# A graph layer on one core: weights in 13 loads instead of 51, blocks laid out on chip, and the first runs' rows turned a run ahead

## The chip, the cores and the metric

The kernel runs on one core of a Trainium2 chip. The metric is the device time of one execution in microseconds, lower is better. A core has five engines with a queue of instructions each: PE (matrix products and transposes), ACT (activations, here mostly copies out of PSUM), DVE (elementwise work), POOL (here: the gathers) and SP (here: issues DMAs). DMAs can be issued from SP, ACT and POOL. Engines wait for one another and for DMAs through semaphores.

## The reference

There are 12,500 nodes with 128 numbers each and 412,500 edges, sorted by destination. Each edge has a source node, 4 attributes (`edge_attr_4`) and 8 radial numbers (`edge_attr_8`).

```python
f0 = x0 @ W1_0e / sqrt(32)                         # x0 = x[:, :32],  x1 = the other 96 as (32, 3)
f1 = einsum('nui,uw->nwi', x1, W1_1o) / sqrt(32)
feat0, self0 = f0[:, :32], f0[:, 32:]              # likewise feat1, self1
e0, e1 = feat0[src], feat1[src]
h = gelu(edge_attr_8 @ W_mlp1 / sqrt(8)); h = gelu(h @ W_mlp2 / sqrt(64))
w00, w01, w10, w11 = h @ Wp_00, h @ Wp_01, h @ Wp_10, h @ Wp_11
mid = products of w.., e0, e1 and the 4 edge attributes        # scalar and vector parts
n0, n1 = segment_sum(mid, dst) / sqrt(32)
conv = n0 @ W2_0e, n1 @ W2_1o (scaled)
out = layernorm(x + cos(pi/8) * self + sin(pi/8) * conv)
```

## The kernel before

**Edges.** The sorted edges are cut into 806 runs of 512 (`SB`), a run into 4 quarters of 128 (one edge per partition), and four runs form a chunk (`CH`).

**Node features.** The features of all nodes are computed once and written to a table in HBM. This is the loop over 25 groups of 512 nodes (`NG`): `load_nodes` brings a group from SP (L156), `turn` transposes it on PE (L180) and ACT copies it into the accumulator `acc` (L181), `features_of` multiplies by the weight `wf` on PE (L187), DVE copies the result (L190), and `store_nodes` writes it to `table` from ACT's queue (L164). Three `xt` and three `ft` buffers and four PSUM buffers `w` let the groups overlap. Half way, `load_indices(0)` turns the source and destination indices of the first 128 runs on PE and DVE.

**Gathers.** `gather(s)` fetches the source rows of a run with one indirect DMA per quarter on POOL (L124), so four per run. It runs up to 19 runs ahead of the work (`LEAD` = 20 buffers `G`). The first 16 runs (`RAW`) don't wait for the table: they gather rows of `x` itself. Their rows are then transposed and multiplied by `wf` when their turn comes, in `features(s)`. In one run of 14 (`AID`), from run 36 on, the fourth quarter is brought by SP instead, as 128 loads of one row (L116).

**The loop over runs.** For run s it does, on PE: now and then a step of the edge MLP (`radial`, `mlp1`, `mlp2`: L347, L356, L371) for a later chunk and `weights` (L388) for two later runs; `segments(s - 1)` (L434), which sums the messages of a run into windows of nodes by a product with the selection `S`; for a raw run `features(s)` (L395 transposes, ACT copy L397, L400 products, ACT copy L402). DVE does `messages(s)` (L422, L425) and `placing(s)`. Per chunk follow `place`, `project` and `add` into `acc`; finished nodes are normalised and stored by `norm`.

**What sets the order.** PE, ACT, DVE and SP execute in the order written in the program (`manual_schedule`); POOL's gathers and a few instructions outside that block, such as the copy of `first_node` (L746), are placed by the scheduler. A `G` buffer becomes free when the last reader is done: for a raw run that is the transposes L395, for another the messages.

**Weights.** `load_wf` fills the block weight `wf` with four loads from ACT's queue, and ACT scales it (L660). `weight_loads` yields 47 more loads (16 of them place `W_mlp1` block by block into `w1b`; the three of `ws` write single floats three apart); the node loop issues three of them from SP per group (L677). After the loop, SP loads the edge data of chunks 1 to 3 (L338) and `aid_rows` (L105), `scale_weights` scales `ws` on ACT and builds `wpost` on DVE, and then come the first steps of the edge MLP, `weights(0)`, `select(0)` and `set_floor`, 25 memsets on DVE (L255, L258), before the loop over runs begins.

Of the kernel before, what the change touches and what calls it, by code (L numbers as in the profile page):

```python
# [49 lines left out]
def gnn_kernel(ctx: ExitStack, tc: tile.TileContext, x, src, dst, ea4, ea8, w1_0, w1_1, wm1, wm2,  # L50
# [114 lines left out]
        if tail:  # L165
            eng.dma_start(dest[n0 + full * P:n0 + nn, :], t[:tail, full, :])

    def load_wf(eng):
        nc.vector.memset(wf, 0.0)
        eng.dma_start(wf[:MUL, :MUL], w1_0[:, :MUL])  # L170
        for i in range(3):
            eng.dma_start(wf[MUL + i::3, MUL + MUL * i:MUL + MUL * (i + 1)], w1_1[:, :MUL])

    XT, PX, PF = {}, {}, {}

# [26 lines left out]
    ones = cst.tile([P, 1], F32)  # L202
    first_node = cst.tile([1, NS], I32)

    def clear():
        for t in (w1b, ws, wpost):
            nc.vector.memset(t, 0.0)
        nc.vector.memset(acc[:, N:], 0.0)
        nc.vector.memset(ones, 1.0)

    def weight_loads():

        for h in range(2):
            for k in range(CH // 2):
                for q in range(Q):
                    r = h * HID + k * Q * RAD + q * RAD
                    yield w1b[r:r + RAD, k * 2 + q // 2, (q % 2) * HID:(q % 2 + 1) * HID], wm1
        for h in range(2):
            rows = slice(h * HID, (h + 1) * HID)
            yield w2b[rows, :], wm2  # L220
            for j, w in enumerate((wp00, wp01, wp10, wp11)):
                yield wpb[rows, j * MUL:(j + 1) * MUL], w
        yield w20[:MUL, :], w2_0[:MUL, :]
        yield w21[:MUL, :], w2_1[:MUL, :]
        for i in range(3):
            r = slice(MUL * (i + 1), MUL * (i + 2))
            yield w20[r, :], w2_0[MUL:, :]
            yield w21[r, :], w2_1[MUL:, :]
        yield first_node, sub(dst, 0, [[1, 1], [SB, NS]])
        yield ws[:MUL, :MUL], w1_0[:, MUL:]  # L230
        for i in range(3):
            yield ws[MUL + i::3, MUL + i::3], w1_1[:, MUL:]

    def scale_weights():
        nc.scalar.mul(ws, ws, math.cos(MIX) / math.sqrt(MUL))
        post = math.sin(MIX) / math.sqrt(2.0) / math.sqrt(NEIGHBORS) / math.sqrt(2 * MUL)
        nc.vector.tensor_scalar(wpost[:MUL, 0, :MUL], w20[:MUL, :], post, None, op0=OP.mult)
        for i in range(3):
            r = slice(MUL * (i + 1), MUL * (i + 2))
            nc.vector.tensor_scalar(wpost[r, 0, MUL + i::3], w21[r, :], post, None, op0=OP.mult)  # L240
            nc.vector.tensor_scalar(wpost[:MUL, 1 + i, MUL + i::3], w21[:MUL, :], post, None, op0=OP.mult)
            nc.vector.tensor_scalar(wpost[r, 1 + i, :MUL], w20[r, :], post / math.sqrt(3.0), None, op0=OP.mult)
# [38 lines left out]
    def load_raws(b):  # L281
        raws[b] = [load_run_rows(dst, b, NO_NODE), load_run_rows(src, b, 0)]
# [42 lines left out]
    def load_edges(b):  # L325
        s0 = b * CH
        ns = min(CH, NS - s0)
        e4[b] = wk.tile([P, CH, Q, 4], F32, name="e4", bufs=EDGES_AHEAD)
        e8[b] = wk.tile([P, CH, Q, RAD], F32, name="e8", bufs=EDGES_AHEAD)
        part = s0 + ns == NS and REM < SB  # L330
        fl = ns - 1 if part else ns
        if part:
            nc.vector.memset(e4[b][:, fl], 0.0)
        if fl < CH:
            nc.vector.memset(e8[b][:, fl:], 0.0)
        for a, t, n in ((ea8, e8[b], RAD), (ea4, e4[b], 4)):
            if fl:
                nc.sync.dma_start(t[:, :fl].rearrange("p s q k -> p (s q) k"),  # L338
                                  sub(a, s0 * SB * n, [[n, P], [P * n, fl * Q], [1, n]]))
            if part and RQ:  # L340
                nc.sync.dma_start(t[:, fl, :RQ, :], sub(a, (s0 + fl) * SB * n, [[n, P], [P * n, RQ], [1, n]]))
            if part and RP:
                nc.sync.dma_start(t[:RP, fl, RQ, :], sub(a, ((s0 + fl) * SB + RQ * P) * n, [[n, RP], [1, n]]))
# [44 lines left out]
                nc.tensor.matmul(WP[i][:, q, :], H2[c][q % 2][rows, k, q // 2, :], wpb[rows, :],  # L388
                                 start=True, stop=True)

    def features(s):

        pt = ps.tile([P, Q, P], F32, name="h")
        for q in range(Q):
            nc.tensor.transpose(pt[:, q, :], G[s][:, q, :], ident)  # L395
        xr = wk.tile([P, Q, P], F32, name="xt", bufs=3)
        nc.scalar.activation(xr, pt, AF.Copy)  # L397
        pf = ps.tile([P, Q, P], F32, name="h")
        for q in range(Q):
            nc.tensor.matmul(pf[:, q, :], xr[:, q, :], wf, start=True, stop=True)  # L400
        G[s] = wk.tile([P, Q, P], F32, name="ft", bufs=3)
        nc.scalar.activation(G[s], pf, AF.Copy)  # L402

# [245 lines left out]

    with tc.manual_schedule(engines={PE, ACT, DVE, SP}):  # L650
        load_raw_rows(nc.sync, 0, min(2, raw_runs))
        load_wf(nc.scalar)
        if raw_runs > 2:
            load_raw_rows(nc.scalar, 2, raw_runs)
        for s in range(min(LEAD - 2, raw_runs)):
            gather(s)
        nc.vector.tensor_scalar(ident, diag, 0.0, None, op0=OP.is_equal)
        for b in range(min(3, NG)):
            XT[b] = load_nodes(b)
        nc.scalar.mul(wf, wf, 1.0 / math.sqrt(MUL))  # L660
        clear()
        nc.vector.memset(odd, 0.0)
        loads = weight_loads()
        for b in range(NG + 2):
            if b == 1:
                load_edges(0)
                load_raws(0)
            if b < NG:
                turn(b)
            if 0 < b <= NG:  # L670
                features_of(b - 1)
            if 1 < b:
                store_nodes(nc.scalar, table, b - 2, PF[b - 2])
            if b + 3 < NG:
                XT[b + 3] = load_nodes(b + 3)
            for _, (to, of) in zip(range(3), loads):
                nc.sync.dma_start(to, of)  # L677
            if b == NG // 2:
                load_indices(0)
        for to, of in loads:  # L680
            nc.sync.dma_start(to, of)
        for c in range(1, min(EDGES_AHEAD, NCH)):
            load_edges(c)
        scale_weights()
        if aided:
            aid_load()
        for s in range(min(LEAD - 2, raw_runs), min(LEAD - 1, NS)):
            gather(s)
        selfs, loaded = list(range(NG)), {}
        radial(0)  # L690
        mlp1(0)
        mlp2(0)
        if NCH > 1:
            radial(1)
            mlp1(1)
        weights(0)
        select(0)
        set_floor()
        for s in range(NS + 1 + CH):
            c, k = divmod(s, CH)  # L700
            if s + LEAD - 1 < NS:
                gather(s + LEAD - 1)
            if k == 3 and c + EDGES_AHEAD < NCH:
                load_edges(c + EDGES_AHEAD)
            if s % P == P // 2 - 16 and (s // P + 1) * P < NS:
                load_raws(s // P + 1)
            if s % P == P // 2 and (s // P + 1) * P < NS:
                load_indices(s // P + 1)
            for t in range(P // ROWS):
                a = s + AID_LEAD - t * STEPS // (P // ROWS)  # L710
                if a in aided:
                    aid(a, t)
            if k == 0 and c + 1 < NCH:
                mlp2(c + 1)
            if k == 1 and c + 2 < NCH:
                radial(c + 2)
            if k % 2 == 0 and s + 2 < NS:
                weights(s + 2)
            if k == 3 and c + 2 < NCH:
                mlp1(c + 2)  # L720
            if k == 2 and 0 < c <= NCH:
                project(c - 1)
            if 0 < s <= NS:
                segments(s - 1)
            if k == 1 and 0 < c <= NCH:
                place(c - 1)
            if s < NS:
                if s < raw_runs:
                    features(s)
                messages(s)  # L730
                placing(s)
            if k == 2 and 0 < c <= NCH:
                add(c - 1)
                norm(due.get(c - 1, []), last=c == NCH)
            if k == 3 and c + 1 < NCH:
                select(c + 1)
            if selfs and s + 8 >= self_from and (s + 8) % self_every == 0:
                b = selfs.pop(0)
                loaded[s + 8] = b, load_nodes(b)
            if s in loaded:  # L740
                self_part(*loaded.pop(s))
        assert not selfs and not loaded
# [41 lines left out]
```

## Time and profile before

| | us |
|---|---|
| median of 3 runs | 6025.94 (6022.07 to 6031.2) |
| the profiled execution | 4038.2 |
| its span, first to last instruction | 4036.1 |
| busy: PE | 3087.6 |
| busy: POOL | 2994.5 |
| busy: DVE | 1718.0 |
| busy: ACT | 1025.7 |
| granted PE clock, mean | 0.761 |

The profile shows one execution, and its time is well under the runs' median. A row of a group gives the line, the engine, the operation, the tile written and the tiles read, the count, the busy time and the mean of one, then the idle time of the engine before it and what ended most of that. In a timeline a row begins with the start and the duration in us; the brackets at its end give the engine's idle time before it and who ended it. An engine name with a q is the engine's queue (SPq: SP issuing DMAs). "issue" is idle time in which the engine waited for nothing that the profile shows.

### The profile page before, as it was taken

What the parts mean: (1) busy time and instruction counts of PE and PEld (TensorE: products, weight loads), DVE (VectorE), ACT (ScalarE), POOL (GpSimd) and SP (SyncE); (2) the same over time, 40 slices, a digit from 0 to 9 for tenths busy, and PEclk for the clock granted to TensorE, in tenths of its full rate; (3) what the DMA queues carried; (4) which work ended last, traced back from release to release, by engine and by line L of the source; (5) the groups of instructions that cost most, each with busy time, mean ns of one, the idle gap of its engine ahead of it and who ended that gap; (6) DMA issues with size and microseconds to landing.
All of it is one profiled execution on the core that took longest, in us unless ns stands there. A gap on an engine that the chain in (4) does not pass through costs nothing.

```text
span 4036.1 us, 82179 instructions
## 1 busy us (share of the span) xinstructions
PE 3087.6 (77%) x25199; PEld 2188.4 (54%) x25199; DVE 1718.0 (43%) x4937; ACT 1025.7 (25%) x2264; POOL 2994.5 (74%) x3176
## 2 busy tenths in 40 slices
PE   5787778777787777778777778877777777777876
PEld 5565455555555555555555555555555555555554
DVE  2354545434444444444344443444444444444343
ACT  2232322322322222222222222222222222222222
POOL 6567777777777777777777777777777777777775
PEclk7787888787877777777777777777777777777776
DMA  8223333333333333333333333333333333333331
GB/s 186 43 53 68 67 73 68 74 68 74 70 69 63 59 66 66 59 66 59 59 64 66 60 62 62 60 64 65 60 64 61 61 60 65 61 60 65 61 59 47
DMA packets 1014835, 265.84 MB, mean 66 GB/s; under 512 B 904975, under 2 KB 962072, under 8 KB 1014386
## 3 DMA queue, kind: packets, MB, share of 16 engines
q0 software_dynamic: 101408, 207.89, 19.9%
q1 hardware_dynamic: 892687, 46.18, 13.8%
q10 hardware_dynamic: 20290, 6.45, 0.6%
q8 instruction: 201, 3.29, 0.3%
q14 instruction: 249, 2.03, 0.2%
HBM read 247.45 MB, written 12.80 MB: 64 GB/s over the span
## 4 chain that ended last, share of the span: by engine, by line
POOL 40%; issue 27%; DMA 11%; PE 10%; DVE 6%; SPq 4%; ACT 2%; DVEq 0%; POOLq 0%; ACTq 0%
POOL G L124 40%; DMA G<-table,idx 9%; SPq L116 2%; PE w L388 2%; DVE M L425 2%; PE seg L434 1%; PE m L459 1%; PE h L371 1%; PE m L451 1%; DMA xt<-in_x 1%; PE m L450 1%; ACT y L520 1%; DVE acc L468 1%; SPq L112 1%; DMA e<-in_edge_attr 1%
## 5 line engine op out<-in xcount | busy, mean ns | idle before, releaser
L124 POOL DMA_INDIRECT G<-table,idx x3105 | 2932.8, 945 | 993.2 <-issue 877.3
L422 DVE TENSOR_TENSOR M<-w,G 128x256 f32<-128x256 f32 x790 | 334.8, 424 | 1800.0 <-DMA G<-table,idx 1600.6
L388 PE MATMUL w<-wpb,h 64*128 64x128 f32 x6448 | 777.0, 358 | 210.1 <-DVE M L425 209.2
L434 PE MATMUL seg<-M,S 128*32 128x256 f32 x6448 | 615.9, 459 | 408.1 <-DVE M L425 393.5
L388 PEld LDWEIGHTS w<-wpb,h 64*128 64x128 f32 x6448 | 633.8, 249 | 371.8 <-DVE M L425 255.0
L425 DVE TENSOR_TENSOR M<-w,G 128x384 f32<-128x384 f32 x1580 | 799.7, 548 | 0.0
L437 ACT ACTIVATE sg<-seg 128x256 f32<-128x256 f32 x806 | 310.5, 385 | 1804.8 <-PE seg L434 1796.3
L451 PE MATMUL m<-pl,sg 128*128 128x96 f32 x1612 | 493.2, 401 | 0.0
L434 PEld LDWEIGHTS seg<-M,S 128*32 128x32 f32 x6448 | 141.7, 117 | 546.9 <-issue 436.9
L371 PE MATMUL h<-h,w2b 64*64 64x256 f32 x3232 | 331.4, 419 | 108.9 <-ACT h L360 102.6
L450 PEld LDWEIGHTS m<-pl,sg 128*128 128x128 f32 x1612 | 350.4, 268 | 113.6 <-issue 85.9
L450 PE MATMUL m<-pl,sg 128*128 128x32 f32 x1612 | 376.2, 322 | 0.0
L459 PE MATMUL m<-st,wpost 128*128 128x128 f32 (+1 forms) x1616 | 374.8, 405 | 1.2 <-ACT st L453 1.2
L451 PEld LDWEIGHTS m<-pl,sg 128*128 128x128 f32 x1612 | 362.3, 277 | 0.0
L459 PEld LDWEIGHTS m<-st,wpost 128*128 128x128 f32 x1616 | 322.8, 297 | 41.8 <-issue 34.7
L371 PEld LDWEIGHTS h<-h,w2b 64*64 64x64 f32 x3232 | 145.4, 141 | 291.7 <-ACT h L360 232.6
L356 PEld LDWEIGHTS h<-eT,w1b 64*128 64x128 f32 x3232 | 233.1, 217 | 121.6 <-issue 110.6
L376 ACT ACTIVATE h<-h 128x512 f32<-128x512 f32 x404 | 219.2, 595 | 260.3 <-PE h L371 260.3
L356 PE MATMUL h<-eT,w1b 64*128 64x128 f32 x3232 | 273.7, 315 | 9.3 <-ACT eT L349 8.3
L443 DVE TENSOR_SCALAR pl<-iota,colv 128x128 f32<-128x128 f32 x806 | 237.0, 294 | 94.3 <-PE m L451 91.5
L360 ACT ACTIVATE h<-h 128x512 f32<-128x512 f32 x404 | 219.2, 594 | 163.6 <-PE h L356 159.0
L453 ACT ACTIVATE st<-m 128x512 f32<-128x512 f32 x202 | 120.4, 596 | 503.4 <-PE m L451 503.4
(101 smaller groups left out, 1178.4 us busy)
## 6 DMA issues: line engine op xcount, KB each, us to landing
G<-table SPq DMA_DIRECT2D x7040, 0.5 KB
G<-table,idx POOLq DMA_INDIRECT x3105
e<-in_edge_attr SPq DMA_DIRECT2D x201, 64.0 KB
xt<-in_x SPq DMA_DIRECT2D x48, 256.0 KB
e<-in_edge_attr SPq DMA_DIRECT2D x201, 32.0 KB
table<-ft ACTq DMA_DIRECT2D x24, 256.0 KB
out<-y SPq DMA_DIRECT2D x24, 256.0 KB
raw<-in_dst SPq DMA_DIRECT2D x6, 256.0 KB
```

The source lines that it names most:

```text
L124: nc.gpsimd.indirect_dma_start(out=G[s][:, q, :], out_offset=None, in_=x if s < raw_runs else table, in_offset=bass.IndirectOffsetOnAxis(a ...
L356: nc.tensor.matmul(p1[h][:, j // 2, j % 2, :], w1b[rows, j, :], eT[c][rows, :], start=True, stop=True)
L371: nc.tensor.matmul(p2[r][k * HID:(k + 1) * HID, h * n:(h + 1) * n], w2b[rows, :], H1[c][h][rows, k * n:(k + 1) * n], start=True, stop=True)
L388: nc.tensor.matmul(WP[i][:, q, :], H2[c][q % 2][rows, k, q // 2, :], wpb[rows, :], start=True, stop=True)
L422: nc.vector.tensor_tensor(m[:, :, :, :MUL], w[:, :, :2 * MUL].rearrange("p q (a u) -> p q a u", a=2), g[:, :, None, :MUL].to_broadcast([P, ...
L425: nc.vector.tensor_tensor(m[:, :, j, MUL:].rearrange("p q (i u) -> p q i u", i=3), w[:, :, None, (2 + j) * MUL:(3 + j) * MUL].to_broadcast ...
L434: nc.tensor.matmul(pt[q * W:(q + 1) * W, :], S[c][:, r * Q + q].rearrange("p k j -> p (k j)"), M[s][:, q].rearrange("p a u -> p (a u)"), s ...
L437: nc.scalar.activation(SG[s], pt, AF.Copy)
L443: nc.vector.tensor_scalar(PL[s], iota, colv[b][:, r:r + 1], None, op0=OP.is_equal)
L450: nc.tensor.matmul(pt[:, k, :W], SG[s][:, :P], PL[s][:, :W], start=True, stop=True)
L451: nc.tensor.matmul(pt[:, k, W:], SG[s][:, P:], PL[s][:, W:], start=True, stop=True)
L459: nc.tensor.matmul(PC[c][:, :ns, :], wpost[:, k, :], ST[c][:, :ns, k, :], start=k == 0, stop=k == 3)
```

## The change

The weights come in 13 loads: two on ACT's queue for `w1`, which holds `W1_0e` and each row of `W1_1o` three times, and eleven on SP, in which a source is repeated over the partitions by a step of 0. `wf`, `ws` and `w1b` are no longer written block by block by DMAs: DVE sums columns of the identity into masks (`comp`, `block`) and multiplies them with the repeated weights, scales included. SP issues one weight load per group from group 5 on. The edge loads, index loads, the builds and the first chunk's `radial`, `mlp1`, `mlp2` are called at fixed groups of the node loop.

`features(s)` is split into `turn_rows(s)` (transposes and the copy) and `features(s)` (products and the copy). Both are called for run s + 1 in iteration s, the turn ahead of `messages(s)`, the products after it; those of run 0 stand before the loop.

```diff
-    def load_wf(eng):
+    def load_w1(eng):
+        eng.dma_start(w1[:MUL, :], w1_0)
+        eng.dma_start(w1[MUL:, :], sub(w1_1, 0, [[2 * MUL, MUL], [0, 3], [1, 2 * MUL]]))
+
+    def make_wf():
+        nc.vector.tensor_reduce(comp, ident[:, MUL:].rearrange("p (u i) -> p i u", i=3),
+                                axis=mybir.AxisListType.X, op=OP.add)
         nc.vector.memset(wf, 0.0)
-        eng.dma_start(wf[:MUL, :MUL], w1_0[:, :MUL])
-        for i in range(3):
-            eng.dma_start(wf[MUL + i::3, MUL + MUL * i:MUL + MUL * (i + 1)], w1_1[:, :MUL])
+        nc.vector.tensor_scalar(wf[:MUL, :MUL], w1[:MUL, :MUL], 1.0 / math.sqrt(MUL), None, op0=OP.mult)
+        nc.vector.scalar_tensor_tensor(wf[:, MUL:].rearrange("p (i c) -> p i c", i=3),
+                                       comp[:, :, None].to_broadcast([P, 3, MUL]), 1.0 / math.sqrt(MUL),
+                                       w1[:, None, :MUL].to_broadcast([P, 3, MUL]), op0=OP.mult, op1=OP.mult)
...
     def weight_loads():
-        for h in range(2):
-            for k in range(CH // 2):
-                for q in range(Q):
-                    r = h * HID + k * Q * RAD + q * RAD
-                    yield w1b[r:r + RAD, k * 2 + q // 2, (q % 2) * HID:(q % 2 + 1) * HID], wm1
...
+        yield w1r, sub(wm1, 0, [[0, P // RAD], [HID, RAD], [1, HID]])
+        yield w2b, sub(wm2, 0, [[0, 2], [HID, HID], [1, HID]])
+        for j, w in enumerate((wp00, wp01, wp10, wp11)):
+            yield wpb[:, j * MUL:(j + 1) * MUL], sub(w, 0, [[0, 2], [MUL, HID], [1, MUL]])
+        for t, w in ((w20, w2_0), (w21, w2_1)):
+            yield t[:MUL, :], w[:MUL, :]
+            yield t[MUL:, :], sub(w, MUL * MUL, [[0, 3], [MUL, MUL], [1, MUL]])
         yield first_node, sub(dst, 0, [[1, 1], [SB, NS]])
-        yield ws[:MUL, :MUL], w1_0[:, MUL:]
-        for i in range(3):
-            yield ws[MUL + i::3, MUL + i::3], w1_1[:, MUL:]
...
+    def make_w1b():
+        nc.vector.tensor_reduce(block, ident.rearrange("p (h m a) -> p m h a", h=2, a=RAD),
+                                axis=mybir.AxisListType.XY, op=OP.add)
+        nc.vector.tensor_tensor(w1b.rearrange("p j (b c) -> p (j b) c", c=HID),
+                                block[:, :, None].to_broadcast([P, 2 * Q, HID]),
+                                w1r[:, None, :].to_broadcast([P, 2 * Q, HID]), op=OP.mult)
...
+        extra = {2: lambda: load_edges(0), 4: lambda: load_raws(0), NG // 2: lambda: load_indices(0),
+                 NG // 2 + 3: make_w1b, NG // 2 + 5: make_ws, NG - 6: lambda: radial(0), NG - 4: lambda: mlp1(0),
+                 NG - 2: lambda: mlp2(0), NG - 1: make_wpost}
         for b in range(NG + 2):
-            if b == 1:
-                load_edges(0)
-                load_raws(0)
...
-            for _, (to, of) in zip(range(3), loads):
-                nc.sync.dma_start(to, of)
-            if b == NG // 2:
-                load_indices(0)
-        for to, of in loads:
-            nc.sync.dma_start(to, of)
+            if b > 4 and loads:
+                nc.sync.dma_start(*loads.pop(0))
+            if b in extra:
+                extra[b]()
...
-        radial(0)
-        mlp1(0)
-        mlp2(0)
         if NCH > 1:
             radial(1)
             mlp1(1)
         weights(0)
         select(0)
+        turn_rows(0)
+        features(0)
         set_floor()
...
+            if s + 1 < raw_runs:
+                turn_rows(s + 1)
             if s < NS:
-                if s < raw_runs:
-                    features(s)
                 messages(s)
                 placing(s)
+            if s + 1 < raw_runs:
+                features(s + 1)
```

More of the change, by code (lines that the diff above doesn't have):

```diff
@@ L166, in store_nodes @@
             eng.dma_start(dest[n0 + full * P:n0 + nn, :], t[:tail, full, :])
-    def load_wf(eng):
+    w1 = cst.tile([P, 2 * MUL], F32)
+    comp = cst.tile([P, 3], F32)
+    def load_w1(eng):
[4 more added lines that the diff above has]
+                                axis=mybir.AxisListType.X, op=OP.add)
         nc.vector.memset(wf, 0.0)
-        eng.dma_start(wf[:MUL, :MUL], w1_0[:, :MUL])
-        for i in range(3):
-            eng.dma_start(wf[MUL + i::3, MUL + MUL * i:MUL + MUL * (i + 1)], w1_1[:, :MUL])
+        nc.vector.tensor_scalar(wf[:MUL, :MUL], w1[:MUL, :MUL], 1.0 / math.sqrt(MUL), None, op0=OP.mult)
+        nc.vector.scalar_tensor_tensor(wf[:, MUL:].rearrange("p (i c) -> p i c", i=3),
+                                       comp[:, :, None].to_broadcast([P, 3, MUL]), 1.0 / math.sqrt(MUL),
+                                       w1[:, None, :MUL].to_broadcast([P, 3, MUL]), op0=OP.mult, op1=OP.mult)
     XT, PX, PF = {}, {}, {}
@@ L203, in gnn_kernel @@
     first_node = cst.tile([1, NS], I32)
+    w1r = cst.tile([P, HID], F32)
+    block = cst.tile([P, 2 * Q], F32)
     def clear():
-        for t in (w1b, ws, wpost):
-            nc.vector.memset(t, 0.0)
+        nc.vector.memset(wpost, 0.0)
         nc.vector.memset(acc[:, N:], 0.0)
         nc.vector.memset(ones, 1.0)
+        nc.vector.memset(odd, 0.0)
     def weight_loads():
-        for h in range(2):
-            for k in range(CH // 2):
-                for q in range(Q):
-                    r = h * HID + k * Q * RAD + q * RAD
-                    yield w1b[r:r + RAD, k * 2 + q // 2, (q % 2) * HID:(q % 2 + 1) * HID], wm1
@@ L218, in weight_loads @@
[L218 to L224, printed above, removed]
-        for i in range(3):
-            r = slice(MUL * (i + 1), MUL * (i + 2))
-            yield w20[r, :], w2_0[MUL:, :]
-            yield w21[r, :], w2_1[MUL:, :]
-        yield first_node, sub(dst, 0, [[1, 1], [SB, NS]])
@@ L230, in weight_loads @@
-        yield ws[:MUL, :MUL], w1_0[:, MUL:]
-        for i in range(3):
-            yield ws[MUL + i::3, MUL + i::3], w1_1[:, MUL:]
-    def scale_weights():
-        nc.scalar.mul(ws, ws, math.cos(MIX) / math.sqrt(MUL))
+        yield w1r, sub(wm1, 0, [[0, P // RAD], [HID, RAD], [1, HID]])
+        yield w2b, sub(wm2, 0, [[0, 2], [HID, HID], [1, HID]])
+        for j, w in enumerate((wp00, wp01, wp10, wp11)):
+            yield wpb[:, j * MUL:(j + 1) * MUL], sub(w, 0, [[0, 2], [MUL, HID], [1, MUL]])
@@ new lines, in make_ws, with make_wpost @@
+    def make_ws():
+        keep = math.cos(MIX) / math.sqrt(MUL)
+        nc.vector.memset(ws, 0.0)
+        nc.vector.tensor_scalar(ws[:MUL, :MUL], w1[:MUL, MUL:], keep, None, op0=OP.mult)
+        nc.vector.scalar_tensor_tensor(ws[:, MUL:].rearrange("p (c i) -> p i c", i=3),
+                                       comp[:, :, None].to_broadcast([P, 3, MUL]), keep,
+                                       w1[:, None, MUL:].to_broadcast([P, 3, MUL]), op0=OP.mult, op1=OP.mult)
+    def make_wpost():
@@ L389, in weights, with turn_rows @@
                                  start=True, stop=True)
-    def features(s):
+    XR = {}
+    def turn_rows(s):
         pt = ps.tile([P, Q, P], F32, name="h")
@@ L395, in features @@
             nc.tensor.transpose(pt[:, q, :], G[s][:, q, :], ident)
-        xr = wk.tile([P, Q, P], F32, name="xt", bufs=3)
-        nc.scalar.activation(xr, pt, AF.Copy)
+        XR[s] = wk.tile([P, Q, P], F32, name="xt", bufs=3)
+        nc.scalar.activation(XR[s], pt, AF.Copy)
+    def features(s):
         pf = ps.tile([P, Q, P], F32, name="h")
         for q in range(Q):
-            nc.tensor.matmul(pf[:, q, :], xr[:, q, :], wf, start=True, stop=True)
+            nc.tensor.matmul(pf[:, q, :], XR[s][:, q, :], wf, start=True, stop=True)
         G[s] = wk.tile([P, Q, P], F32, name="ft", bufs=3)
@@ L651, in gnn_kernel @@
         load_raw_rows(nc.sync, 0, min(2, raw_runs))
-        load_wf(nc.scalar)
+        load_w1(nc.scalar)
         if raw_runs > 2:
@@ L659, in gnn_kernel @@
             XT[b] = load_nodes(b)
-        nc.scalar.mul(wf, wf, 1.0 / math.sqrt(MUL))
+        make_wf()
         clear()
-        nc.vector.memset(odd, 0.0)
-        loads = weight_loads()
+        loads = list(weight_loads())
+        extra = {2: lambda: load_edges(0), 4: lambda: load_raws(0), NG // 2: lambda: load_indices(0),
+                 NG // 2 + 3: make_w1b, NG // 2 + 5: make_ws, NG - 6: lambda: radial(0), NG - 4: lambda: mlp1(0),
+                 NG - 2: lambda: mlp2(0), NG - 1: make_wpost}
         for b in range(NG + 2):
-            if b == 1:
-                load_edges(0)
-                load_raws(0)
             if b < NG:
@@ L675, in gnn_kernel @@
                 XT[b + 3] = load_nodes(b + 3)
-            for _, (to, of) in zip(range(3), loads):
-                nc.sync.dma_start(to, of)
-            if b == NG // 2:
-                load_indices(0)
-        for to, of in loads:
-            nc.sync.dma_start(to, of)
+            if b > 4 and loads:
+                nc.sync.dma_start(*loads.pop(0))
+            if b in extra:
+                extra[b]()
+        assert not loads
         for c in range(1, min(EDGES_AHEAD, NCH)):
             load_edges(c)
-        scale_weights()
         if aided:
```

## The prediction

> **What bounds the kernel now.** I read the page from the busy shares to the chain, then followed the engine that leads both. POOL and PE are both near 75% busy, but the chain that ended last names POOL and the pauses between its instructions ("issue"):
>
> ```profile
> PE 3087.6 (77%) x25199; PEld 2188.4 (54%) x25199; DVE 1718.0 (43%) x4937; ACT 1025.7 (25%) x2264; POOL 2994.5 (74%) x3176
> POOL 40%; issue 27%; DMA 11%; PE 10%; DVE 6%; SPq 4%; ACT 2%; DVEq 0%; POOLq 0%; ACTq 0%
> L124 POOL DMA_INDIRECT G<-table,idx x3105 | 2932.8, 945 | 993.2 <-issue 877.3
> ```
>
> One gather is 945 ns and is followed by 0.30 us of "issue", so POOL's pace is 1.25 us a gather, 4.99 us a run of four. There are 3105 + 64 = 3169 gathers: 3169 x 1.248 = 3955 us. The first starts at 3.36, the last at 4008.36, 4005.0 us later, and the span ends 27.7 us after that. So POOL idles beyond its pace for only about 46 to 50 us in the whole execution. POOL's waits from 80 to 232 us (columns: total us, times, longest) say where:
>
> ```profile
> POOL G L124 <- PE h L395: 40.3, 14, 6.2
> POOL G L124 <- DMA e<-in_edge_attr: 8.9, 1, 8.9
> POOL G L124 <- DVE M L425: 1.7, 1, 1.7
> ```
>
> Less the 0.30 that every gather has anyway, that is 36.1 + 8.6 + 1.4 = **46.1 us**. POOL's timeline dates them (start, duration, idle before):
>
> ```profile
> 82.38 0.94 POOL L124 DMA_INDIRECT G<-in_x,idx_raw  x1 [0.30 <-issue]
> 92.24 0.94 POOL L124 DMA_INDIRECT G<-table,idx  x1 [8.92 <-DMA e<-in_edge_attr]
> ...
> 123.95 0.94 POOL L124 DMA_INDIRECT G<-table,idx  x1 [2.02 <-PE h L395]
> ...
> 229.94 0.94 POOL L124 DMA_INDIRECT G<-table,idx  x1 [1.65 <-DVE M L425]
> ```
>
> The 64 gathers of raw rows end at 83.3 and the table is not complete until 92.2. From run 22 on each gather needs a G buffer (20 of them) that the raw runs free only when PE has turned their rows (L395). After 229.94 POOL never waits longer than 0.6 us. A microsecond is gained only where POOL idles before 230.
>
> What makes the raw runs late is the start of the loop and their pace. The timeline of SP and DVE:
>
> ```profile
> 50.01 5.06 SPq L677 DMA_DIRECT2D ws<-in_L_gnn_W_1o  x3
> 76.97 11.05 SPq L338 DMA_DIRECT2D e<-in_edge_attr  x6
> ...
> 97.06 0.30 DVE L409 TENSOR_TENSOR m<-iota,rel 128x128 f32<-128x128 f32 x1 [5.80 <-ACT eT L349]
> ...
> 106.00 5.13 DVE L258 MEMSET floor<- 1x470 f32 x14 [0.15 <-DVE floor L258]
> 111.18 0.41 DVE L422 TENSOR_TENSOR M<-w,ft 128x256 f32<-128x256 f32 x1
> ```
>
> Node loads end at 76.5, SP then issues edge loads for 11 us, the first MLP stages follow on PE and ACT, `select(0)` starts at 97.06, and the floor memsets keep DVE until the first message at 111.18. From there the turns of runs 2 to 15 start at 122.56 to 222.95: 7.72 us a run against POOL's 4.99.
>
> [...] each `ws` load (1024 single floats) holds SP for 0.71 to 3.51 us, a `w2b` load of 64 rows about 0.55. [...] granted clock 0.78 from 121 to 230 us, 1.00 from 230 to 260, and eight products of L400 last 1.17 or 2.08 us.
>
> **The change, part by part.** *Loads.* 47 loads on SP (L677) become 11, and 4 on ACT become 2. SP's issue durations for those removed: 16 `w1b` x 0.30, 8 `wpb` x 0.60, 8 `w20`/`w21` x 0.48, 2 `w2b` x 0.55, 4 `ws` about 5.4, so about 20 us; the 10 new weight loads at 0.5 to 0.6 cost 5 to 6; `first_node` stays at 0.92. About 14 us of SP's issue goes. It lay between node loads, which PE waited for (L180 on xt: 23.4 us idle, 11 times), but the DMA share is already 0.75 to 1.0 in most of that stretch, so not all comes off. The edge and index loads move from step 1 to steps 2 and 4, behind the first six node loads instead of four: they still cost their issue (3.61 + 2.29 us). From 60 to 80 us, with no weight loads, groups go by at 2.0 us each. 25 such groups are 50; starting at 5, plus 6 to 8 for the index transposes, 1 to 3 for the edge and row loads, the last node load is issued at about 63 instead of 76.5: **13 us earlier, bounds 5 and 18**.
>
> *Building on DVE.* Two reductions, the products and memsets for w1b, ws, wf: about 3.5 us by the nearest rows (128x512 product 0.69, memset 0.17 to 0.48); they replace about 1 us of memsets and two ACT scalings (0.31 each). wf must wait for w1's two loads; before it waited for four and was ready at 8.05. Hidden in a DVE busy 6 us in 20 (60 to 80). The copy of `first_node` stays in DVE's order and now sits two instructions after the load's step; before, issue to landing was 6.7 us, and DVE waited 2.9. Behind it stand the feature copies and so the table stores; I count up to 4 us more, inside the bounds above.
>
> *First MLP stages moved into the node loop.* radial(0), mlp1(0), mlp2(0) held PE and ACT from 90.2 to 95.7 after the last store; moved between node groups they cost 5 us of PE there, mostly beside DMA. radial(1) and `select(0)` follow the stores directly: **6.5 us** off the way to `select(0)`. It starts at 97.06 - 13 - 6.5 = 77.6, and the first message, 14.1 us later as now, at 91.7. The table is ready at 92.2 - 13 = 79, ahead of 83.3: the 8.6 us wait goes.
>
> *Rows turned a run ahead.* Run 1 is turned before the first message, run 2 about 2.4 us after it: 94.1 to 95.2. In the built order turn(s+1) and features(s+1) still stand together on PE, so PE keeps waiting for the ACT copy between them (10.4 us, 14 times); what goes are its waits for messages, 7.0 before the segments and 4.5 before the weights. 109 us of raw stretch less 11.5 is 97.5, or 6.9 us a run; [...] so I take 6.5, bounds 5.7 and 7.3. Run 15 is turned at 95.2 + 13 x 6.5 = 179.7. POOL at its pace wants that buffer at 3.36 + 35 x 4.99 = 178.0, and run 16's, freed by its messages some 6.6 us after the turn, at 183.0: wait 3.3. **Sum: 46.1 - 3 = 43 us**, between 28 (both bounds bad) and 46. The tail of 27.7 us is untouched, and nothing else on POOL changes.
>
> *Against the times.* The profiled execution took 4038.2 us (span 4036.1), so it would take 3995. The median of the runs is 6025.94, 1988 us longer, and no view shows where those lie. If they are outside this stretch, 43 come off: **5983**. If every piece is stretched by 1.49, 64 do: 5962.
>
> **The rivals.** *The runs gather more slowly.* If the 1988 us lie in the gathers, each takes 1.25 + 1988/3169 = 1.88 us. The raw gathers then end at 124, after the table's 92, and run 22's buffer is wanted at 3.4 + 88 x 1.88 = 169, when it was free at 124: POOL has no idle time to win, time 6026 (6014 to 6032). For it: a bound by gathers[...]. Against it: gathers here are 938 to 1358 ns, median 944, in all 4 ms. *It half works*: DMA sets the node loop, 28 us or less: 5998 to 6012. *Slower:* [...] The raw pace alone saves 16 us, so the start must come 16 us later than now, 36 later than worked out: from 5 us per load on. For 12 us of loss it takes 7. Time 6040. The removed loads landed without holding SP that long, which speaks against it. *The change doesn't do what it says*: turns and products stay adjacent on PE; that is in the 6.5.
>
> **The numbers.** Full gain 0.51, stretched 0.08, half 0.06, slow gathers 0.24, slower 0.11. Forecast 5983. The likeliest case alone spans 5979 to 5998; the range reaches to the stretched case and to no change, 5955 to 6030. A measurement of this kernel tells about 0.2%, 12 us, from no change. Faster by more 0.65, within 0.24, slower 0.11.
>
> **What would show it.** Right: the first table gather 0.30 us after the last raw one; POOL's wait for the turns under 10 us in total instead of 40.3; the first message near 92; last gather near 3965 in the profile. Wrong: table later than 83; raw runs at over 7.3 us; or a profile 43 us shorter beside an unmoved median.

## The result, and the profile after

The changed kernel took 5985.03 us, median of 11 runs (5974.26 to 6017.13), against 6022.69 for the kernel before (11 runs). The ratio is 0.9952, 95% interval 0.9931 to 0.9973: **38 us faster**, two microseconds from the forecast of 5983. The number was right, though those two microseconds are luck: the kernel before measured 6022.69 here and 6025.94 then, and the interval alone allows a gain of 16 to 42 us. Half of the reasoning under it was not right, as the page of the changed kernel shows at once. Here are its busy times, its chain and its costliest group (count, busy time and mean, then idle time before and what ended most of it), as shown of before:

```profile
PE 3220.7 (54%) x25199; PEld 2267.2 (38%) x25199; DVE 1693.3 (28%) x4943; ACT 1024.6 (17%) x2262; POOL 2992.1 (50%) x3176
...
PE 24%; another core or an unknown queue 23%; issue 5%; ACT 5%; DVE 2%; SPq 0%; DVEq 0%; DMA 0%; ACTq 0%
...
L124 POOL DMA_INDIRECT G<-table,idx x3105 | 2930.6, 944 | 2910.9 <-DVE pl L465 1470.7
```

This execution took 6014.41 us, not some 3995. A gather is as short as before (944 ns), but POOL idles 2910.9 us ahead of its gathers, 1967 more than its pace takes, and half of that for DVE's `placing`, not for its own next issue. POOL bounds nothing here.

Both pages are right: the same kernel runs at two levels. Each comparison ran on one chip, and all its runs, of both kernels, agreed on a level: the kernel before took 6023 to 6027 us in two comparisons (the chip of one of them is on record) and 4035 to 4041 in three others, on three further chips. The level goes with the chip as far as this shows; no chip on record was tried twice. The profile of before that the prediction was read from (4038.2) is of the lower level, the medians beside it and the profile just shown are of the upper. The changed kernel at the lower level is the fair partner of the profile of before: it took 4000.84 against 4040.99, ratio 0.9898 (0.9881 to 0.9914), **40 us faster** where the working said 43. Its page:

```profile
PE 3066.0 (77%) x25199; PEld 2169.9 (54%) x25199; DVE 1718.7 (43%) x4943; ACT 1024.8 (26%) x2262; POOL 3001.8 (75%) x3176
...
POOL 32%; DMA 20%; issue 20%; SPq 10%; PE 10%; DVE 5%; ACT 2%; DVEq 0%; POOLq 0%; ACTq 0%
...
L124 POOL DMA_INDIRECT G<-table,idx x3105 | 2939.9, 947 | 947.5 <-issue 806.8
```

POOL leads the chain again, with DMA and "issue" behind it. POOL's waits from 80 to 232 us (total, times, longest), the first three rows, and POOL's timeline around the table and at the end:

```profile
POOL G L124 <- issue: 30.9, 101, 0.4
POOL G L124 <- DMA G<-table,idx: 2.7, 9, 0.3
POOL G L124 <- DVE M L447: 0.9, 3, 0.3
...
POOL G L124 <- PE h L414: 0.6, 2, 0.3
```

```profile
83.31 0.95 POOL L124 DMA_INDIRECT G<-in_x,idx_raw  x1 [0.30 <-issue]
84.66 0.94 POOL L124 DMA_INDIRECT G<-table,idx  x1 [0.40 <-issue]
...
3970.76 0.95 POOL L124 DMA_INDIRECT G<-table,idx  x1 [0.30 <-issue]
```

The wait for the turns (now L414), 40.3 us before, is 0.6. The first table gather follows the last raw one by 0.40, where it stood 8.92. No wait in this stretch is longer than 0.4. The last gather starts at 3970.76 (forecast 3965) instead of 4008.36.

### The profile page after: what moved, and what is told of

Its sections match the earlier page's. It is cut to its first block, busy times and chain, and to the rows that moved or that the text cites. A ratio compares the mean times of both kernels' runs of the same rounds, so it can differ in the third digit from the quotient of the medians.

```text
span 6012.6 us, 82144 instructions
## 1 busy us (share of the span) xinstructions
PE 3220.7 (54%) x25199; PEld 2267.2 (38%) x25199; DVE 1693.3 (28%) x4943; ACT 1024.6 (17%) x2262; POOL 2992.1 (50%) x3176
## 3 DMA queue, kind: packets, MB, share of 16 engines
q0 software_dynamic: 101408, 207.89, 13.4%
## 4 chain that ended last, share of the span: by engine, by line
PE 24%; another core or an unknown queue 23%; issue 5%; ACT 5%; DVE 2%; SPq 0%; DVEq 0%; DMA 0%; ACTq 0%
PE seg L456 4%; PE w L405 4%; PE m L473 4%; PE m L481 4%; PE m L472 3%; PE h L388 3%; PE h L373 2%; ACT h L393 1%; ACT h L377 1%; ACT sg L459 1%; ACT y L542 0%; PE m L364 0%; DVE M L447 0%; DVE acc L490 0%
## 5 line engine op out<-in xcount | busy, mean ns | idle before, releaser
L124 POOL DMA_INDIRECT G<-table,idx x3105 | 2930.6, 944 | 2910.9 <-DVE pl L465 1470.7
L456 PE MATMUL seg<-M,S 128*32 128x256 f32 x6448 | 667.5, 491 | 1845.4 <-ACT sg L459 1479.0
L405 PE MATMUL w<-wpb,h 64*128 64x128 f32 x6448 | 693.5, 373 | 16.1 <-issue 15.9
L405 PEld LDWEIGHTS w<-wpb,h 64*128 64x128 f32 x6448 | 588.6, 267 | 154.8 <-issue 151.0
L388 PE MATMUL h<-h,w2b 64*64 64x256 f32 x3232 | 365.4, 473 | 351.8 <-ACT h L377 318.1
L473 PE MATMUL m<-pl,sg 128*128 128x96 f32 x1612 | 550.0, 442 | 0.0
L481 PE MATMUL m<-st,wpost 128*128 128x128 f32 (+1 forms) x1616 | 388.9, 416 | 146.9 <-ACT st L475 133.2
L472 PEld LDWEIGHTS m<-pl,sg 128*128 128x128 f32 x1612 | 404.8, 308 | 164.6 <-issue 117.0
L490 DVE TENSOR_TENSOR acc<-m,acc 128x32 f32 x806 | 154.5, 192 | 1072.8 <-PE m L481 402.4
L472 PE MATMUL m<-pl,sg 128*128 128x32 f32 x1612 | 424.3, 355 | 10.7 <-ACT eT L366 5.9
L473 PEld LDWEIGHTS m<-pl,sg 128*128 128x128 f32 x1612 | 413.3, 314 | 0.0
L388 PEld LDWEIGHTS h<-h,w2b 64*64 64x64 f32 x3232 | 159.8, 158 | 542.1 <-ACT h L377 456.1
```

The costliest lines, as they stand in the source:

```text
L124: nc.gpsimd.indirect_dma_start(out=G[s][:, q, :], out_offset=None, in_=x if s < raw_runs else table, in_offset=bass.IndirectOffsetOnAxis(a ...
L388: nc.tensor.matmul(p2[r][k * HID:(k + 1) * HID, h * n:(h + 1) * n], w2b[rows, :], H1[c][h][rows, k * n:(k + 1) * n], start=True, stop=True)
L456: nc.tensor.matmul(pt[q * W:(q + 1) * W, :], S[c][:, r * Q + q].rearrange("p k j -> p (k j)"), M[s][:, q].rearrange("p a u -> p (a u)"), s ...
L472: nc.tensor.matmul(pt[:, k, :W], SG[s][:, :P], PL[s][:, :W], start=True, stop=True)
L473: nc.tensor.matmul(pt[:, k, W:], SG[s][:, P:], PL[s][:, W:], start=True, stop=True)
L481: nc.tensor.matmul(PC[c][:, :ns, :], wpost[:, k, :], ST[c][:, :ns, k, :], start=k == 0, stop=k == 3)
```

## The experiments

"Level" below is the time of the kernel before in the same comparison: about 6025 is the upper, about 4035 the lower. Gaps are stretches of over 6 us between two starts on PE (products or weight loads), counted in the trace. Theories A to D are named in the expectations.

**Where do 1988 us lie? The kernel before, unaltered, profiled again (one run).**

> The kernel before, unchanged, for a trace that stands beside the changed kernel's. If the long idle times of PE (once in about 250 PE instructions, 12 us each, some 200 of them) belong to ordinary executions and not to the change, this trace has some 200 of them too, a span near 6010 us and POOL idle over 2500 us. If they came with the change, the span is near 4036 us again and POOL waits only before 230 us.

6050.37 us, and a trace like that of the changed kernel: 204 gaps, together 2443 us, about one per chunk of four runs. (The profile of before at the lower level has 26, together 197 us.) POOL's waits in it:

```profile
POOL G L124 <- DVE pl L443: 1459.4, 291, 8.5
POOL G L124 <- issue: 853.7, 2684, 8.8
POOL G L124 <- DVE M L425: 428.1, 71, 13.6
```

So the long waits were there before the change, and the 1988 us are pauses of PE spread over the whole loop, not a lump outside the stretch that the change touches.

**The loads alone, 6027 level (22 runs).** `features` as before; loads, builds and early MLP stages as changed.

```diff
-            if s + 1 < raw_runs:
-                turn_rows(s + 1)
             if s < NS:
+                if s < raw_runs:
+                    turn_rows(s)
+                    features(s)
                 messages(s)
                 placing(s)
-            if s + 1 < raw_runs:
-                features(s + 1)
```

> The 13 loads, the builds on DVE and the earlier MLP stages, but turns and products of a raw run together in its own iteration as before. Prediction's theory (the start of the loop and POOL's pace decide): most of the 38 us, ratio 0.995 to 0.997. Rival (PE's idle times decide, and what counts is PE's waiting in the raw stretch): the loads hide behind PE's idle times, ratio 0.999 to 1.001.

6026.46 against 6027.17, ratio 0.9991 (0.9975 to 1.0007): nothing that can be told, as the rival had it. The prediction's theory wanted 0.995 to 0.997.

**The turn a run ahead alone, 6027 level (15 runs).** The opposite mixture: the loads of before, with `features` split as in the change and this edit to its loop.

```diff
+            if s + 1 < raw_runs:
+                turn_rows(s + 1)
             if s < NS:
-                if s < raw_runs:
-                    features(s)
                 messages(s)
                 placing(s)
+            if s + 1 < raw_runs:
+                features(s + 1)
```

> The 51 loads as before, the raw rows turned a run ahead. Prediction's theory: 11 to 18 us from a raw stretch of 6.5 to 6.9 instead of 7.7 us a run, ratio 0.997 to 0.998. Rival (PE decides): the same PE waits go, about 11 us of messages waited for, and more where a PE idle time overlaps them, ratio 0.994 to 0.998.

6005.40 against 6027.17, ratio 0.9947 (0.9928 to 0.9966), as much as the whole change (0.9952), and more than the 0.997 to 0.998 that the prediction's theory gave this part. In the traces the placings of runs 2 to 15 take 109 us before, 110 with the loads alone, 88 with the turn alone and 88 with both.

**Does a PE gap come with a number of PE instructions? (one run)**

```diff
+        for i in runs:
+            rows = slice((i - s) * HID, (i - s + 1) * HID)
+            for _ in range(3):
+                nc.tensor.matmul(WP[i][:1, 0, :1], H2[c][0][rows, k, 0, :1], wpb[rows, :1], start=True, stop=True)
```

> The changed kernel with three further products of 1x1 per run ahead of the weights, overwritten by them: 806 x 3 x 4 = 9672 more PE instructions[...]. If PE idles once in so many instructions (250), the number of its idle times over 6 us rises from 203 to about 240, and the time by 37 x 12 = 0.44 ms besides. If it idles once in a chunk of four runs, for a reason in the chunk's work, the number stays near 203.

6212.31 us, 4836 more product instructions on PE (30,035 instead of 25,199, half the 9672 that the expectation counted) and yet 188 gaps, where one per so many instructions would give about 240. They don't come with a count of PE's instructions.

**Pauses on POOL: three versions that met the other level (4 runs each).** The question was whether long unbroken trains of gathers cause the gaps of PE. A memset on POOL after each gather (128 and 384 columns) or two of 768 columns after each run was to break them up.

```diff
+    pause = cst.tile([P, 128], F32)
...
                 in_offset=bass.IndirectOffsetOnAxis(ap=rows, axis=0))
+            nc.gpsimd.memset(pause, 0.0)
```

> The changed kernel with one POOL memset of 128 columns after every gather, into a tile that nobody reads. From the 0.23 us of the 128-column IOTA it should lengthen POOL's pace from 1.25 to about 1.48 us a gather, 5.9 us a run. Theory A (a train of gathers issued back to back holds up PE's signals to ACT and DVE until the train ends; PE starts fall from 9 to under 1 per us from the fourth us of a train of twelve): the pauses let the signals through if the spacing is what counts, the 200 PE gaps of over 6 us shrink to under 100 and the time falls below 5900. If only an empty queue lets them through, the gaps stay and the time is within 1% of 5985. Theory B (the gaps are PE's, ACT's or SP's own, once a chunk, and POOL merely fills them): 200 gaps and 5985 within 0.5%, since POOL idles 1967 us in the changed kernel and the pauses take some 730. Theory C (POOL's pace bounds, as the prediction had it): 3169 x 0.23 = 730 us more, 6715.

> As the run before with 384 columns: a pace of about 1.73 us a gather by estimate from the 0.10 us of a one-column memset and the 0.23 us of the 128-column IOTA, 6.8 us a run. Theory A: fewer gaps than with 128 columns, under 60; the time then follows POOL, 806 x 6.8 + some 150 at the start, 5630 to 5800. Theory B: 200 gaps and 5985, or more where POOL now comes late. Theory C: 3169 x 0.48 = 1520 us more, 7500.

> The same total of pause in one piece: two memsets of 768 columns after the four gathers of a run, about 1.7 us, 6.7 us a run. Theory A, spacing between single gathers counts: gaps stay near 200, no faster than 5985. Theory A, the length of the train counts (trains of 3 and 4 gathers leave PE at 4 to 5 starts per us and never stop it; those of 11 and 12 do): gaps under 60 and a time of 5600 to 5800. Theory B: 200 gaps, 5985 or more.

The kernel before took 4034.62 here, so the baseline of 5985 in all three texts was not there, and theory A had no gaps to shorten. The three took 4841.36 (ratio 1.1999, 1.1979 to 1.2019), 5494.67 (1.3616, 1.3593 to 1.3639) and 5247.38 (1.3004, 1.2982 to 1.3025). The pauses also did not stand where they were meant to: nothing tied them to the gathers, and the scheduler drew them forward in POOL's order (the last of 3169 with 128 columns starts at 1610 us), so that run 200 was placed at 1846 us and the rest followed at 4.9 us a run. Their sum still tells something. The group of the memsets with 128 columns (busy, mean, idle before):

```profile
L129 POOL MEMSET pause<- 128x128 f32 x3169 | 651.0, 205 | 172.9
```

651.0 + 172.9 = 824 us. The changed kernel itself did not run in this comparison; by its ratio of 0.9898 it would take some 3993 us, and the kernel with pauses took 848 more. With 384 columns 1329 + 166 = 1495 us were put on POOL and cost 1501, with 768 per run 1193 + 80 = 1273 cost 1254. Theory C's mechanism holds in these three runs, to within 3%: what their memsets put on POOL was paid in full.

**Without SP's rows (4 runs, same comparison).**

```diff
-    aided = range(AID_FROM, NS - 1, AID)
+    aided = range(AID_FROM, AID_FROM)
```

> The changed kernel without the rows that SP brings: 7040 loads of one row on SP go, 55 gathers come to POOL. Theory A: the trains grow no shorter, about 200 gaps, time within 1.5% of 5985, 69 us more at most (55 x 1.25). Rival D (SP's row loads, 0.73 us apart in the gaps instead of 0.32, cause the gaps): under 50 gaps and a time below 5000. Theory C: 69 us more, 6054.

4058.57 against 4034.62, ratio 1.0056 (1.0039 to 1.0073). Less 55 gathers of 1.248 us this is 3989.9, which says without a run of it what the changed kernel should take at this level. Rival D could not be judged by this run, since there were no gaps to lose.

**The changed kernel at the 4041 level (4 runs).**

> The changed kernel unaltered, since the kernel before took 6023 us in one comparison and 4035 in another. Where the kernel before takes about 4035: if POOL's pace bounds and the turn a run ahead and the earlier table together take away its idle time, as forecast, the changed kernel takes 4035 - 43 = 3992; the run without SP's rows says the same (4058.6 less 55 gathers of 1.248 us = 3990). If the loads bring nothing there either, some 4013. Where the kernel before takes about 6023: 5985, as it did, with some 200 PE gaps of over 6 us.

4000.84, ratio 0.9898, shown above: 40 us where the first case has 43. By the ratios (1.0056 without SP's rows, on another chip) the 55 gathers cost about 65 us, with an uncertainty of 10; POOL's pace says 69.

**Pauses tied to the gathers (4 runs, same comparison).**

```diff
+            nc.gpsimd.memset(G[s][:, q, :], 0.0)
             nc.gpsimd.indirect_dma_start(
                 out=G[s][:, q, :], out_offset=None, in_=x if s < raw_runs else table,
```

> The changed kernel with a memset of 128 columns on POOL into the G buffer ahead of every gather. The memsets of the earlier run had no tie to the gathers and were placed early, all within the first 220 runs; these stay with their gathers. From the 0.255 us a gather that the earlier run added, POOL's pace is 1.50 us, 5.9 us a run. Where the kernel before takes about 4035 (POOL bounds): 3990 + 3169 x 0.255 = 4800. Where it takes about 6023: Theory A, spacing counts: gaps of PE shrink to under 100 and the time falls below 5700; Theory A, the train's length alone, or Theory B (the gaps are PE's, ACT's or SP's own): about 200 gaps, 5985 within 1%; Theory C, POOL's pace adds up: 6780.

4418.24, ratio 1.0933 (1.0915 to 1.0951). The level was again the lower one; the cost is 417 us over the changed kernel, 0.13 a gather instead of 0.255. The memsets take 584.7 us together, where 3169 of 223 ns would take 707, so they overlap, and the idle time ahead of the table's gathers falls from 947.5 to 774.6 (its "issue" from 806.8 to 499.5): they partly lie in what was "issue" before. Theory A stays untested.

**Each part alone at the 4036 level (9 runs of the loads, 4 of the turn).**

> The loads, builds and the earlier MLP stages without the turn a run ahead, once more. Where the kernel before takes about 4040: the loop starts some 14 us earlier (first placing 98 instead of 112 us in the changed kernel) but runs at 7.7 us a raw run, so the last raw buffer is late by 46 - 17 = 29 us instead of 46: a gain of 17 us, ratio 0.9957. If the loads bring nothing, 1.000. Where it takes about 6023: 0.999 as before.

> The turn a run ahead without the loads, once more. Where the kernel before takes about 4040: the loop starts as late as before, at 112 us, and then places runs 2 to 15 at 5.5 us each, as the changed kernel does, instead of 7.6: 13 x 2.1 = 28 us of the 46 go, ratio 0.9931. The two parts together make the 40 us only if both are needed. Where it takes about 6023: 0.995 as before.

Loads alone: 4025.98, ratio 0.9973 (0.9963 to 0.9983), 10 us. Turn alone: 3995.46, ratio 0.9898 (0.9883 to 0.9913), 41 us. The expectation for the turn was 28 us, and wrong in a telling way: the turn needs no help from the loads. The transposes of run 15 start at 180.62 instead of 222.65, 42 us earlier. The pace, 5.46 us a run instead of 7.70, makes 29 of these; the other 13 were left out of the expectation: with run 1 turned ahead of the first message, run 2 starts at 109.58 instead of 122.56. POOL's waits from 70 to 260 us with the loads alone, then the first table gather with the turn alone:

```profile
POOL G L124 <- PE h L414: 33.2, 12, 6.4
POOL G L124 <- issue: 31.4, 102, 0.6
POOL G L124 <- DMA G<-table,idx: 3.1, 10, 0.3
POOL G L124 <- DVE M L447: 2.6, 4, 1.6
```

```profile
88.39 0.94 POOL L124 DMA_INDIRECT G<-table,idx  x1 [5.00 <-DMA e<-in_edge_attr]
```

POOL's idle time beyond 1.248 us a gather, from the starts of the gathers in each trace:

| us | at the table, 80 to 100 | turns, 100 to 235 | after 235 | last gather starts |
|---|---|---|---|---|
| before | 8.6 | 37.9 | 4.5 | 4008.36 |
| loads alone | 0.0 | 31.3 | 5.6 | 3995.14 |
| turn alone | 4.7 | 0.3 | 4.7 | 3967.30 |
| both | 0.2 | 0.4 | 11.9 | 3970.76 |

There were 46.5 us to win up to 235. The loads alone win 15 of them, the turn alone 41.5, both 45.9. These are single traces, from more than one chip: 3.9 of the 41.5 stand at the table, where the turn changes nothing, so the shares hold to about 4 us. What both gain over the turn alone (4 us at the table) is lost after 235, where a gather has a mean of 947 ns instead of 945; that execution is from the chip on which the kernel before is also 5 us slower (4041 against 4036), so I put it to the chip, without having tried it.

No version beats the changed kernel; the turn alone equals it.

## Why the prediction was right or wrong

**The bound.** At the level of the profile that it was read from it was right: POOL's pace of 1.25 us a gather, shown by pauses that cost what POOL spends on them, and in keeping with 55 gathers that cost about 65. At the level of the medians it was wrong. The step that failed is "if they are outside this stretch, 43 come off". They are inside it, and everywhere else.

**The loads.** SP's side was sized well. The last node load is issued at 65.19, forecast 63, before 76.5. The table is no longer waited for, though it is used at 84.66, later than the 79 of the forecast and than the 83 that was to prove it wrong; it costs 0.1 us, because the last raw gather starts only at 83.31. The ten new weight loads held SP for 9.0 us, not 5 to 6. The kernel before has 39 loads at L677, not 47, and 43 in all, not 51: the forecast's list adds up to 38 and `first_node`, and its 20 us come from the list, so nothing else changes. The rival of loads landing so late that SP stands still at each fell: at the lower level the loads alone are faster, at the upper no slower that can be told.

**The first MLP stages.** `select(0)` was forecast at 77.6 and the first message at 91.7; they came at 82.88 and 97.05. The step that failed is "radial(1) and `select(0)` follow the stores directly". SP's timeline, then DVE's:

```profile
65.94 12.08 SPq L355 DMA_DIRECT2D e<-in_edge_attr  x6
78.08 2.35 SPq L105 DMA_DIRECT2D aid_rows<-in_src  x1
```

```profile
82.74 0.31 DVE L106 TENSOR_SCALAR aid_at<-aid_rows 55x128 int32<-55x128 int32 x1 [4.88 <-DMA aid_rows<-in_src]
82.88 0.36 DVE L431 TENSOR_TENSOR m<-iota,rel 128x128 f32<-128x128 f32 x1
...
97.05 0.41 DVE L444 TENSOR_TENSOR M<-w,ft 128x256 f32<-128x256 f32 x1
```

Ahead of `select(0)` in DVE's order stands the scaling of `aid_rows`, a load that SP issues behind 12 us of edge loads. That wait of 4.88 us took the place of the work moved away. In before the same scaling came at 91.04 and was hidden: `select(0)` then still waited 5.80 us for ACT. The forecast had moved the stages and not looked at what else was queued behind the same point.

**The rows a run ahead.** The forecast was 6.5 us a run, bounds 5.7 and 7.3; the transposes of runs 3 to 15 start from 106.29 to 171.06, 64.77 us for 12 runs, **5.40 us a run**, outside the bounds (before: 122.56 to 222.65 for 13, 7.70). PE's waits, first in before (122 to 230 us), then in the changed kernel (106 to 171):

```profile
PE h L400 <- ACT xt L397: 10.4, 14, 0.7
PE seg L434 <- DVE M L425: 7.0, 6, 2.1
PE w L388 <- DVE M L425: 4.5, 3, 1.7
```

```profile
PE h L422 <- ACT xt L416: 9.0, 12, 0.7
PE h L373 <- ACT ft L424: 1.0, 3, 0.3
```

The two waits for messages are gone and the one for the ACT copy stays at 0.75 a run, both as forecast. They are worth 11.5 / 13 = 0.9 us a run, and the gain is 7.70 - 5.40 = 2.3. The mis-sized term is the clock, which the forecast put at 0.4 (from 6.9 to 6.5) by estimate; in before it was 0.78 with PE busy 78% of the time (121 to 230 us) and 1.00 with PE busy 97% (230 to 260). The busy times of the raw stretch (window; its length; PE, PEld, DVE, ACT and POOL busy with counts; granted clock; DMA share; GB/s), before and changed:

```profile
100.00:230.00 130.00, 96.24 (x699) 70.53 (x699) 42.22 (x114) 37.87 (x75) 69.84 (x75) 0.76 0.22 42
```

```profile
97.00:176.00 79.00, 64.71 (x587) 46.48 (x587) 31.99 (x87) 30.63 (x62) 59.64 (x63) 0.94 0.27 57
```

The granted clock rose from 0.76 to 0.94. Per run PE is busy 96.24 x 7.70 / 130 = 5.7 us before and 64.71 x 5.40 / 79 = 4.4 after, 1.3 us less for nearly the same work (41 and 40 PE instructions a run); with the 0.9 that makes 2.2 of the 2.3. The clock goes with the turn and not with the loads, as the raw stretch shows with the loads alone, then with the turn alone:

```profile
97.00:213.00 116.00, 90.73 (x611) 66.53 (x610) 28.70 (x80) 33.85 (x66) 65.20 (x70) 0.74 0.20 42
```

```profile
109.00:185.00 76.00, 62.88 (x580) 45.81 (x572) 29.49 (x79) 30.17 (x61) 57.41 (x62) 0.96 0.28 57
```

In before the eight products of L400 last 2.07 us about once per chunk, in the changed kernel for the last time at 101.27 and 1.16 in every later run. The clock records in the traces show what came just ahead of it: in before the clock falls from 1.00 to 0.50 at 141.8, 172.5 and 203.3, each time 0.7 to 1.4 us after the end of a wait of 2.1 us by PE for a message (the longest wait of the second row above), and stays there for 13.7 us. In the changed kernel that wait is gone, and the clock is halved at 97.0 for the last time in the raw stretch. That the wait brings the half clock is read from these three cases, not shown. If it does, the waits removed from PE paid twice here: 0.9 us a run of waiting and 1.3 of busy time.

**The sum.** 46.1 - 3 = 43 against 40.2. Run 15 is turned at 171.06, 7 us ahead of POOL's wish at 178.0, so the residual wait of 3.3 is nil. That 43 came so near is partly luck: the first message was 5.4 us later than forecast and the pace 1.1 us a run faster, and of the 45.9 us won up to 235 some 7 were lost after it. The forecast added the loads and the turn as if both were needed. Each eats from the same 46 us; the turn alone takes nearly all of it, and the loads then have nothing left to win.

**The medians.** There the 38 us have another path. The loop over nodes is stretched as well: its last load is issued at 131.67, before at 134.85, and POOL still waits for the table, 64.0 us against 67.2. The placing of run 16 comes at 277 us instead of 307 in the profiles, and that of the last run at 5989 instead of 6023. The loads alone advance run 16 by 6 us. So some 30 us are won by the end of the raw stretch. That they are kept because PE, not POOL, sets the end fits the page, whose chain names PE and not POOL; two traces can't show it, since single executions of the kernel before lie between 5999 and 6067. The stretched rival (64 us) overstated it: of the 109 us for these 13 runs 21 came off. The rival of slow gathers had the right doubt, that the 1988 us sit in the stretch, and the wrong place for it: gathers last 944 to 947 ns at both levels.

**What the 1988 us are** is only half known. One pause in the changed kernel at the upper level, PE, then ACT, then POOL:

```profile
2079.06 1.04 PE L456 MATMUL seg<-M,S 128*32 128x256 f32 x8
2080.03 0.33 PE L364 MATMUL m<-ident,e 128*128 128x128 f32 x1
2093.67 0.66 PE L456 MATMUL seg<-M,S 128*32 128x256 f32 x4 [13.31 <-ACT sg L459]
```

```profile
2093.23 0.38 ACT L459 ACTIVATE sg<-seg 128x256 f32<-128x256 f32 x1 [14.97 <-remote]
```

```profile
2076.02 0.94 POOL L124 DMA_INDIRECT G<-table,idx  x1 [4.38 <-DVE pl L465]
...
2089.77 0.94 POOL L124 DMA_INDIRECT G<-table,idx  x1 [0.30 <-issue]
```

PE's products end by 2080.4 in the profile and ACT has only to copy them, but the semaphore that PE counts up is next recorded at 2093.21. "remote" says that the profile finds no one who released ACT. In this trace some 400 of the 2854 updates of that semaphore are recorded over 5 us after PE's instruction (each matched with the next update on record); in the changed kernel at the lower level it is one. Meanwhile POOL issues twelve gathers without a pause. Counting gathers that start within 1.4 us of each other as a train, PE's starts fall under two per us from four us after the start of a train of twelve and come back some two us after its end (127 trains); in trains of four (157) they stay above four while the train lasts. That PE's signals are held up while POOL's gathers run on is what this suggests. It is not shown. The ends of PE's products are modelled, so PE itself may have stood still in them; POOL may also have long trains only because buffers have piled up; and at the lower level POOL issues over 3000 gathers without a pause while PE has only 23 gaps, of 8 us each.

Three rivals can be judged from the traces. SP's row loads (rival D) aren't needed for a gap: in 28 of the 203 gaps of the changed kernel no row load starts, and five of these 28 lie before 95 us, while the first row load comes at 278. Loads of instructions, counted as the packets of queue q8, of kind "instruction", don't set the number of gaps: there are 201 at both levels, and 239 in the kernel with the extra products, which has fewer gaps (188). Nor do slower transfers: the packets of the gathers' queue took 13.4% of 6013 us, 806, and in before at the lower level 19.9% of 4036, 803. The runs meant to separate cause from effect all met the lower level, so the cause stays open, and so does whether it is the chip itself.

## What to carry to other kernels

When a profile's own time is a third below the runs' median, profile once more before working out a bound: the two were at different levels here, and a forecast read from one held on the other only because the stretch it touched was slow on both. Two edits that shorten the same idle time don't add; build each alone. And when a wait is taken from PE, price the granted clock of the stretch as well as the wait (0.76 to 0.94 here).

## What was not expected of the hardware

The same kernel took 4035 to 4041 us on three chips and about 6025 in two comparisons, one of them on a fourth chip, with gathers of 944 to 947 ns on all. A granted clock of 0.76 became 0.94 when about 0.9 us of waiting per run of 7.7 us was taken from PE.
